# Attention over sixteen images: one image's score chunks, value projection and value products in another order

## The chip, the cores and the metric

The kernel runs on one core of a Trainium2 chip. The time is that of the device for one execution, in microseconds (us); a kernel is run several times and its median is given. A separate execution is recorded by the hardware profiler; it has a time of its own and a span, which is the stretch from the first to the last recorded instruction.

The engines are TensorE (PE in the profile, its weight loads PEld), VectorE (DVE), ScalarE (ACT), GpSimd (POOL) and SyncE (SP, which issues DMAs). Each has a queue of its own.

## What is computed

Four layers follow each other on x of shape (16, 256, 28, 28) in float32. The first is a 3x3 convolution of signs with batch norm, the second a gated block with a 3x3 and a 1x1 convolution, the third has two 3x3 convolutions of signs with batch norms. The change lies in the fourth, an attention within each image, with N = 28 * 28 = 784 positions and 64 reduced channels:

```python
xf = x.reshape(B, C, N)
q = jnp.einsum('rc,bcn->bnr', Wq, xf)
k = jnp.einsum('rc,bcn->brn', Wk, xf)
v = jnp.einsum('rc,bcn->bnr', Wv, xf)
scale = 1.0 / jnp.sqrt(jnp.float32(k.shape[1]))
attn = jnp.einsum('bnr,brm->bnm', q, k) * scale
attn = jax.nn.softmax(attn, axis=-1)
out = jnp.einsum('bnm,bmr->brn', attn, v)
out = jnp.einsum('cr,brn->bcn', Wp, out)
return out.reshape(B, C, H, W) + x
```

## The kernel before

The layers are stages, one after the other on the one core. The images stay in SBUF between the last two stages, as 128 partitions x 2 channel blocks x 784 positions each. The attention is `attend_unshifted` (L1242), some 280 us at the end of the span. It begins with the third layer's last batch norm and activation, which `finish_a` (L1283, ScalarE, with a GpSimd DMA that adds the residual from DRAM) and `finish_b` (L1290, VectorE) apply image by image.

An image's keys are cut into seven chunks of 112 positions, padded to 128 rows. For each chunk, `scores(b, c)` (L1326) multiplies keys by queries with two matmuls of 64 rows, one in the upper and one in the lower half of the array, into a pair of PSUM banks (pool `ps_sc`, two pairs). ScalarE takes the exponential of the 128 x 784 result into one of seven SBUF buffers `es` (L1335). The softmax is not shifted by its maximum.

- `queries_keys` (L1305) makes queries and keys of an image with full 128 x 128 matmuls into the bank pair `mi`; `keys_to` (L1317) and `queries` (L1312) copy them out, on ScalarE and VectorE.
- `project_v` (L1389) makes the values with tiles of 128 rows and 32 columns into bank `sm`; a ScalarE copy goes to `vt`, and `turn_v` (L1403, VectorE) transposes it.
- `values(b, c)` (L1356) multiplies a chunk's exponentials by its values with tiles of 128 x 64, accumulating over the seven chunks in bank `av`. `take_values` (L1364, ScalarE) copies the sum out.
- `sum_up` (L1337) adds exponentials of chunks, those of chunks 0 to 3 on GpSimd and 4 to 6 on VectorE; `sum_all` (L1347, VectorE) joins both; `denominators` (L1369) sums over the partitions by matmuls with ones, again 128 x 64, into bank `sm`; `invert` (L1377) and `normalize` (L1380) are on VectorE. `watch` (L1384, ScalarE) keeps sums for a check of range.
- `project(b, mo)` (L1406) makes one half of the output channels with 64-row matmuls into `mi`, and VectorE adds the result to the image (L1423). `store` (L1443) writes the image out by a DMA of SP.

In the trace one float32 matmul appears as two, so that one score chunk or one half of a projection is x4.

The order on PE, ScalarE, VectorE and GpSimd is that of the calls, written out by hand: `tc.manual_schedule` (L1449) keeps each engine's instructions as the program issues them. The loop over images (L1469) interleaves three images: scores of image b, queries, keys and values of image b + 1, denominators of b - 1 and projections of b - 2. `project(b - 2, ...)` is done only for b > 1, and `take_values(b - 1)` and `denominators(b - 1)` only for b > 0. The last image has its own code (L1520 and below), which stays as it is.

Of the kernel before, what the change touches and what calls it, by code (L numbers as in the profile page):

```python
# [1220 lines left out]
def two_banks(pool, tag):  # L1221
    return pool.tile([P, 2, 512], F32, tag=tag, name=tag)
# [19 lines left out]
def attend_unshifted(ctx, tc, d, out, wqk, wv, wp, keys, worst, doubts, flag, pv, finish):  # L1242
# [31 lines left out]
    def buf(name, bufs, dt=F32, shape=(P, 2, HN)):  # L1274
        return ph.tile(list(shape), dt, tag=name, name=name, bufs=bufs)
# [7 lines left out]
    def finish_a(b, n=slice(0, N), ks=range(2)):  # L1283
        for k in ks:
            v = x[b][:, k, n]
            A.activation(v, v, AF.Identity, bias=bg3[:, k:k + 1], scale=sg3[:, k:k + 1])
        if b >= 2 and 1 in ks:
            nc.gpsimd.dma_start(out=x[b], in_=x2d[b], accum_op=ALU.add)

    def finish_b(b, n=slice(0, N), ks=range(2)):  # L1290
        for k in ks:
            v = x[b][:, k, n]
            if b < 2:
                V.tensor_tensor(v, v, x2[b][:, k, n], ALU.add)
            V.scalar_tensor_tensor(v, v, alpha[:, k:k + 1], v, ALU.mult, ALU.max)  # L1295

    def keep_busy(n):

        ps = one_bank(pssm, "sm")
        for _ in range(n):  # L1300
            T.matmul(ps, lhsT=idle[:, 0:P], rhs=idle, start=True, stop=True)
# [3 lines left out]
    def queries_keys(b, h, ps):  # L1305

        for k in range(2):
            T.matmul(  # L1308
                ps[:, h, :HN], lhsT=wqk[:, k, :], rhs=x[b][:, k, h * HN:(h + 1) * HN], start=(k == 0), stop=(k == 1)
            )  # L1310

    def queries(b, h, ps):  # L1312
        if h == 0:
            qs[b] = buf("q", 2, shape=(P, HN))
        A.copy(qs[b][64 * h:64 * h + 64], ps[0:64, h, :HN])  # L1315

    def keys_to(b, rows, h, ps):  # L1317
        copy = A.copy if rows else V.tensor_copy
        copy(  # L1319
            keys[b % 2][64 * rows:64 * rows + 64, :, 2 * h:2 * h + 2, 0:GC].rearrange("p c g i -> p g c i"),  # L1320
            ps[64:P, h, :HN].rearrange("p (g c i) -> p g c i", g=2, i=GC),
        )
# [3 lines left out]
    def scores(b, c):  # L1326
        ps = two_banks(pssc, "sc")
        chunk = keys[b % 2].rearrange("p c g i -> p c (g i)")[:, c, :]
        for h in range(2):
            rows = slice(64 * h, 64 * h + 64)  # L1330
            T.matmul(  # L1331
                ps[:, h, :HN], lhsT=chunk[rows], rhs=qs[b][rows], start=True, stop=True
            )
        e = es[b, c] = buf("es", 7)
        A.activation(e, ps[:, :, :HN], AF.Exp, scale=0.125)  # L1335

    def sum_up(b, *cs):  # L1337

        for c in cs:
            late, e = c > 3, es[b, c]  # L1340
            if c in (1, 5):
                sums[b, late] = buf(f"sum{c}", 2)
                (V if late else nc.gpsimd).tensor_tensor(sums[b, late], es[b, c - 1], e, ALU.add)
            elif c in (2, 3, 6):
                (V if late else nc.gpsimd).tensor_tensor(sums[b, late], sums[b, late], e, ALU.add)  # L1345
# [18 lines left out]
    def take_values(b, n=slice(0, HN)):  # L1364
        if n.start == 0:
            os[b] = (buf("o", 2, shape=(P, HN)), buf("r", 2, shape=(P, HN)))
        A.copy(os[b][0][:, n], avs[b][:, n])
# [12 lines left out]
    def normalize(b, n=slice(0, HN)):  # L1380
        o, r = os[b]
        V.tensor_tensor(o[:, n], o[:, n], r[:, n], ALU.mult)
# [20 lines left out]
    def turn_v(b):  # L1403
        V.transpose(va[b % 2].rearrange("p c r -> p (c r)"), vt.rearrange("p c a i -> p (c a i)"))
# [38 lines left out]
    def store(b, mo=slice(0, 2), queue=nc.sync):  # L1443
        queue.dma_start(out=out[b][:, mo], in_=x[b][:, mo])
# [4 lines left out]
    with tc.manual_schedule(engines={ET.PE, ET.Activation, ET.DVE, ET.Pool}):  # L1449

        ps = [two_banks(psmi, "mi"), two_banks(pssc, "sc")]
        for h in range(2):
            n = slice(h * HN, h * HN + HN)
            finish_a(0, n)
            finish_b(0, n)
            queries_keys(0, h, ps[h])
        keep_busy(8)
        for h in range(2):
            keys_to(0, 1, h, ps[h])
            queries(0, h, ps[h])  # L1460
            keys_to(0, 0, h, ps[h])
        finish_a(1)
        scores(0, 0)
        project_v(0)
        finish_b(1, ks=(0,))
        turn_v(0)
        finish_b(1, ks=(1,))
        V.transpose(ones.rearrange("p a i -> p (a i)"), turned.rearrange("p a i -> p (a i)"))
        for b in range(B - 1):  # L1469
            scores(b, 1)  # L1470
            if b > 0:
                take_values(b - 1)
            if b == 0:
                finish_a(2)
            if b > 1:
                project(b - 2, 0)()
            sum_up(b, 1)
            scores(b, 2)
            if b > 0:
                sum_up(b - 1, 6)  # L1480
            scores(b, 3)
            sum_up(b, 2, 3)
            ps = two_banks(psmi, "mi")
            for h in range(2):
                queries_keys(b + 1, h, ps)
            for h in range(2):
                keys_to(b + 1, 1, h, ps)
            for h in range(2):
                queries(b + 1, h, ps)
            for h in range(2):  # L1490
                keys_to(b + 1, 0, h, ps)
            project_v(b + 1)
            if b > 0:
                sum_all(b - 1)
            turn_v(b + 1)
            scores(b, 4)
            scores(b, 5)
            sum_up(b, 5)
            if b + 2 < B:
                finish_b(b + 2)  # L1500
            if b + 3 < B:
                finish_a(b + 3)
            for c in range(4):
                values(b, c)
            if b > 0:
                denominators(b - 1)
                invert(b - 1)
                normalize(b - 1)
            scores(b, 6)
            scores(b + 1, 0)  # L1510
            if b > 1:
                project(b - 2, 1)()
                store(b - 2)
            if b > 0:
                watch(b - 1)
            for c in range(4, NC_):
                values(b, c)


        b = B - 1  # L1520
        scores(b, 1)
        take_values(b - 1)
        project(b - 2, 0)()
        sum_up(b, 1)
        scores(b, 2)
        denominators(b - 1)
        invert(b - 1)
        scores(b, 3)
        sum_up(b, 2, 3)
        normalize(b - 1)  # L1530
        scores(b, 4)
        scores(b, 5)
        sum_up(b, 5)
        scores(b, 6)
        project(b - 2, 1)()
        store(b - 2)
        doubts_so_far()
        for mo in range(2):
            project(b - 1, mo, pool=pssc)()
        store(b - 1)  # L1540
        watch(b - 1)
        for c in range(3):
            values(b, c)
        denominators(b)
        for c in range(3, NC_):
            values(b, c)

        parts = [slice(0, HN // 2), slice(HN // 2, HN)]
        os[b] = (buf("o", 2, shape=(P, HN)), buf("r", 2, shape=(P, HN)))
        r = os[b][1]  # L1550
        watched = [worst[:, i:i + 1] for i in range(4 * b, 4 * b + 4)]
        junk = buf("junk", 1, shape=(P, HN))
        A.activation(junk, dns[b], AF.Copy, accum_out=watched[0])
        for n in parts:
            invert(b, n)
        A.activation(junk[:, parts[0]], r[:, parts[0]], AF.Copy, accum_out=watched[1])
        V.tensor_reduce(watched[2], r[:, parts[1]], AX.X, ALU.add)
        A.copy(os[b][0], avs[b][:, :HN])
        up = raise_flag(two_banks(psmi, "mi")[:, 0, :])
        for n in parts:  # L1560
            normalize(b, n)
        up()

        adds = [
            project(b, mo, ps, n) for n, mo, ps in (
                (parts[0], 0, two_banks(psmi, "mi")),
                (parts[0], 1, two_banks(pssc, "sc")),
                (parts[1], 0, [one_bank(pssm, "sm"), one_bank(psav, "av")]),
                (parts[1], 1, two_banks(pssc, "sc")),
            )  # L1570
        ]
        for add in adds[0::2]:
            add()
        store(b, slice(0, 1), nc.scalar)
        for add in adds[1::2]:
            add()
        store(b, slice(1, 2), nc.scalar)
# [178 lines left out]
```

## Time and profile before

| what | value |
|---|---|
| median of 3 runs | 975.81 us (974.52 to 977.21) |
| profiled execution, its own time | 975.5 us |
| its span | 973.7 us |
| mean granted TensorE clock | 0.994 |
| PE busy | 944.8 us (97%) |
| DVE busy | 773.4 us (79%) |
| ACT busy | 722.3 us (74%) |
| POOL busy | 141.0 us (14%) |
| exponentials, L1335 | 112 of 822 ns each |
| score matmuls, L1331 | 448 of 513 ns each, in pairs side by side |
| value and denominator matmuls into `av`, L1352 | 448 of 499 ns each, in pairs |
| reciprocal, L1378, 128x392 | 2608 ns each |

How to read it: a line of the timeline gives the start in us from the span's start, the busy length in us, the engine, the line of the kernel, the operation, the tile that is written and those that are read, the shapes, and how many instructions are merged (x8). For matmuls, "64*128" is the part of the array that one matmul uses, rows times columns. In brackets stands the idle time of that engine just before the group, and what ended it. The ends of matmuls are modelled, and matmuls side by side overlap, so a run of matmuls is best measured from its start to the start of the next run.

### The profile page before, as it was taken

What the parts mean: (1) busy time and instruction counts of PE and PEld (TensorE: products, weight loads), DVE (VectorE), ACT (ScalarE), POOL (GpSimd) and SP (SyncE); (2) the same over time, 40 slices, a digit from 0 to 9 for tenths busy, and PEclk for the clock granted to TensorE, in tenths of its full rate; (3) what the DMA queues carried; (4) which work ended last, traced back from release to release, by engine and by line L of the source; (5) the groups of instructions that cost most, each with busy time, mean ns of one, the idle gap of its engine ahead of it and who ended that gap; (6) DMA issues with size and microseconds to landing.
All of it is one profiled execution on the core that took longest, in us unless ns stands there. A gap on an engine that the chain in (4) does not pass through costs nothing.

```text
span 973.7 us, 14804 instructions
## 1 busy us (share of the span) xinstructions
PE 944.8 (97%) x5615; PEld 582.8 (60%) x5615; DVE 773.4 (79%) x1417; ACT 722.3 (74%) x1199; POOL 141.0 (14%) x149
## 2 busy tenths in 40 slices
PE   7999899999999999999999999999999999999996
PEld 3555568877887878887555555555444444444443
DVE  4767878899998889985799997999757777777765
ACT  6787468888888888874788868887676767666652
POOL 3000100000000000000100000000054444444431
PEclk9999999999999999999999999999999999999998
DMA  9877513334443222110490000000044353525212
GB/s 347 312 271 270 197 50 99 116 115 131 146 152 117 100 100 96 58 63 34 180 383 1 1 1 1 1 1 1 1 71 96 72 129 70 130 67 133 67 67 103
DMA packets 26948, 105.82 MB, mean 109 GB/s; under 512 B 3490, under 2 KB 7268, under 8 KB 26868
## 3 DMA queue, kind: packets, MB, share of 16 engines
q1 hardware_dynamic: 20948, 73.44, 21.2%
q0 software_dynamic: 5632, 30.54, 11.6%
q8 instruction: 46, 0.75, 0.3%
q10 hardware_dynamic: 288, 0.80, 0.2%
q14 instruction: 34, 0.28, 0.1%
HBM read 72.67 MB, written 32.11 MB: 108 GB/s over the span
## 4 chain that ended last, share of the span: by engine, by line
PE 46%; DVE 3%; ACT 1%; issue 1%; DVEq 0%; ACTq 0%
PE cv L340 19%; PE sc L1331 8%; PE av L1352 8%; PE mi L1308 4%; PE sm L1394 2%; PE mi L1412 2%; PE sm L1352 1%; DVE p L1118 1%; DVE ab L354 0%; ACT es L1335 0%; DVE l2b_fin L1120 0%; DVE l2c_fin L1120 0%; DVE r L1378 0%; DVE p L1295 0%; PE sc L1412 0%
## 5 line engine op out<-in xcount | busy, mean ns | idle before, releaser
L340 PE MATMUL cv<-fpads,wpk 128*128 128x392 f16 (+1 forms) x1746 | 295.7, 331 | 10.2 <-ACT fpads L451 5.0
L713 PE MATMUL cv<-vs,w 128*128 128x392 bf16 (+1 forms) x1536 | 287.1, 356 | 2.9 <-DVE vs L134 2.7
L340 PEld LDWEIGHTS <-wpk 128*128 128x128 f16 x1746 | 169.0, 97 | 137.3 <-issue 9.9
L713 PEld LDWEIGHTS cv<-vs,w 128*128 128x128 f32 x768 | 142.6, 190 | 11.7 <-ACT vs L695 0.7
L1335 ACT ACTIVATE es<-sc 128x784 f32<-128x784 f32 x112 | 87.3, 822 | 41.4 <-PE sc L1331 41.4
L713 PEld LDWEIGHTS <-w 128*128 128x128 f16 x768 | 67.7, 101 | 58.1 <-issue 18.5
L1331 PE MATMUL sc<-q,keyswa 64*128 64x392 f32 x448 | 89.9, 513 | 0.9 <-ACT es L1335 0.9
L1118 DVE SCALAR_TENSOR_TENSOR p<-ab,vec 128x392 f32<-128x392 f32 x128 | 79.1, 618 | 2.3
L1352 PE MATMUL av<-es,v 128*64 128x392 f32 x448 | 80.7, 499 | 0.0
L1345 POOL TENSOR_TENSOR sum<-sum,es 128x784 f32<-128x784 f32 x32 | 67.2, 2100 | 3.1 <-ACT es L1335 0.6
L1331 PEld LDWEIGHTS sc<-q,keyswa 64*128 64x128 f32 x448 | 38.9, 186 | 44.0 <-issue 17.1
L851 POOL DMA_DIRECT2D x2d<-x x16 | 8.6, 537 | 343.9 <-DVE x L845 280.9
L1319 DVE COPY keyswa<-mi 64x392 f32<-64x392 f32 x31 | 16.3, 564 | 52.6 <-ACT q L1315 52.5
L1352 PEld LDWEIGHTS av<-es,v 128*64 128x64 f32 x448 | 29.4, 136 | 47.4 <-issue 47.0
L695 ACT CAST vs<-vs 128x840 fp32r<-128x840 bf16 x64 | 54.7, 882 | 1.5 <-DVE vs L134 1.5
L351 ACT ACTIVATE t<-cv,rounding 128x392 f32<-128x392 f32 (+2 forms) x82 | 51.6, 630 | 4.9 <-PE cv L340 1.9
L1123 ACT ACTIVATE t<-ab 128x392 f32<-128x392 f32 x64 | 33.5, 524 | 27.9 <-DVE ab L354 27.9
L823 PE MATMUL cv<-z,fw 128*128 128x392 f32 x256 | 48.9, 342 | 1.0 <-ACT z L815 0.8
L354 DVE SCALAR_TENSOR_TENSOR ab<-ab,cv 128x392 f32<-128x392 f32 x64 | 35.5, 554 | 17.5 <-ACT ab L352 17.5
L823 PEld LDWEIGHTS cv<-z,fw 128*128 128x128 f32 x256 | 45.7, 188 | 2.3 <-ACT z L815 2.1
L1308 PE MATMUL mi<-p,wqk 128*128 128x392 f32 x124 | 45.3, 506 | 0.3 <-DVE p L1295 0.3
L432 PE MATMUL unused<-idle 128*128 128x512 bf16 x175 | 40.5, 389 | 3.0 <-POOL idle L468 3.0
(287 smaller groups left out, 1511.4 us busy)
## 6 DMA issues: line engine op xcount, KB each, us to landing
xs<-in_x_dram SPq DMA_DIRECT2D x30, 784.0 KB, 5.8
x2d<-x POOLq DMA_DIRECT2D x16, 784.0 KB, 3.8
out_dram<-p SPq DMA_DIRECT2D x15, 784.0 KB, 3.8
p<-x2d POOLq DMA_DIRECT2D x14, 784.0 KB, 6.9
p<-x2d SPq DMA_DIRECT2D x13, 784.0 KB, 16.1
n0d<-n POOLq DMA_DIRECT2D x16, 392.0 KB, 4.7
n<-n0d SPq DMA_DIRECT2D x16, 392.0 KB, 3.3
st<-in_w_dram SPq DMA_DIRECT2D x12, 384.0 KB, 6.1
```

Of the source, the lines that this page charges most:

```text
L340: T.matmul(pss[j][:, n // size if careful else h, :rows * S].rearrange("p (a b) -> p a b", b=S), lhsT=w[:, n, t, :], rhs=pads[:, blocks[j] ...
L351: A.activation(by_halves(t, blocks[j]), ps, AF.Identity, bias=rounding, scale=1.0 / PACK)
L432: tc.keep_in_program_order(T.matmul(ps, lhsT=idle[:, 0:P], rhs=idle, start=True, stop=True))
L695: A.copy(v, w)
L713: T.matmul(ps.rearrange("p (a b) -> p a b", b=S), lhsT=w[:, k, c, u, mo * P:(mo + 1) * P], rhs=v[:, b % 2, u, k, :, c:c + S], start=(n == ...
L823: T.matmul(ps[:, h, :HN], lhsT=w[:, k, mo * P:(mo + 1) * P], rhs=z2[b][:, k, h * HN:(h + 1) * HN], start=(k + i == 0), stop=(k + i == 2),)
L1118: V.scalar_tensor_tensor(p, y, alpha[:, mo:mo + 1], y, ALU.mult, ALU.max)
L1308: T.matmul(ps[:, h, :HN], lhsT=wqk[:, k, :], rhs=x[b][:, k, h * HN:(h + 1) * HN], start=(k == 0), stop=(k == 1))
L1331: T.matmul(ps[:, h, :HN], lhsT=chunk[rows], rhs=qs[b][rows], start=True, stop=True)
L1335: A.activation(e, ps[:, :, :HN], AF.Exp, scale=0.125)
L1345: (V if late else nc.gpsimd).tensor_tensor(sums[b, late], sums[b, late], e, ALU.add)
L1352: T.matmul(ps[64 * h:64 * h + 64, :HN], lhsT=w, rhs=e[:, h, :], start=start, stop=stop)
```

## The change

Only the order of calls in the loop over the images changes. Chunk 4's scores move from behind `turn_v` to the score chunks 1 to 3; chunk 2's scores move ahead of the first projection; chunk 5's scores move behind the denominators, to chunk 6; the second projection moves between chunk 6's scores and the next image's chunk 0; `sum_up(b, 5)` moves behind that projection. So no scores stand any more between the value projection and the value products. Calls, buffers and shapes are the same.

```diff
             if b == 0:
                 finish_a(2)
+            scores(b, 2)
             if b > 1:
                 project(b - 2, 0)()
             sum_up(b, 1)
-            scores(b, 2)
+            scores(b, 3)
             if b > 0:
                 sum_up(b - 1, 6)
-            scores(b, 3)
+            scores(b, 4)
             sum_up(b, 2, 3)
             ps = two_banks(psmi, "mi")
...
             if b > 0:
                 sum_all(b - 1)
             turn_v(b + 1)
-            scores(b, 4)
-            scores(b, 5)
-            sum_up(b, 5)
             if b + 2 < B:
                 finish_b(b + 2)
             if b + 3 < B:
                 finish_a(b + 3)
             for c in range(4):
                 values(b, c)
             if b > 0:
                 denominators(b - 1)
                 invert(b - 1)
                 normalize(b - 1)
+            scores(b, 5)
             scores(b, 6)
-            scores(b + 1, 0)
             if b > 1:
                 project(b - 2, 1)()
                 store(b - 2)
+            sum_up(b, 5)
+            scores(b + 1, 0)
             if b > 0:
                 watch(b - 1)
             for c in range(4, NC_):
                 values(b, c)
```

## The prediction

> **What bounds the kernel now.** I read the windows first. From 737.58 to 934.47 us, twelve images of the attention, TensorE is busy for the whole stretch, at full clock; VectorE (DVE), ScalarE (ACT) and GpSimd (POOL) have room.
>
> ```profile
> 737.58:934.47 196.89, 196.89 (x1298) 91.57 (x1297) 146.62 (x144) 132.17 (x226) 83.81 (x48) 1.00 0.38 95
> ```
>
> The columns are length, busy time of PE, PEld, DVE, ACT and POOL, clock, DMA share, GB/s. A busy PE can still be slow where one kind of matmul follows another, so I then read PE's timeline over one image. A run ends where the next line starts; the second column overlaps the next run a little.
>
> ```profile
> 797.52 0.93 PE L1331 MATMUL sc<-q,keyswa 64*128 64x392 f32 x4
> 798.29 0.84 PE L1412 MATMUL mi<-o,wp 64*128 64x392 f32 x4
> 798.96 1.48 PE L1331 MATMUL sc<-q,keyswa 64*128 64x392 f32 x8
> 800.37 2.90 PE L1308 MATMUL mi<-p,wqk 128*128 128x392 f32 x8
> 803.21 1.53 PE L1394 MATMUL sm<-p,wv 128*32 128x196 f32 x32
> 804.67 1.59 PE L1331 MATMUL sc<-q,keyswa 64*128 64x392 f32 x8
> 806.19 2.85 PE L1352 MATMUL av<-es,v 128*64 128x392 f32 x16
> 808.87 0.83 PE L1352 MATMUL sm<-sum,ones 128*64 128x392 f32 x4
> 809.63 1.59 PE L1331 MATMUL sc<-q,keyswa 64*128 64x392 f32 x8
> 811.05 0.82 PE L1412 MATMUL mi<-o,wp 64*128 64x392 f32 x4
> 811.80 2.19 PE L1352 MATMUL av<-es,v 128*64 128x392 f32 x12
> ```
>
> x4 is one score chunk (or one half of a projection), x8 two, in the tiling written as rows*columns. The next image begins at 813.93: 16.41 us each. There are seven runs of one tiling: 64*128, 128*128, 128*32, 64*128, 128*64, 64*128, 128*64.
>
> Third, ACT over the same image, because each score chunk needs an exponential before its bank pair is free again, and there are two pairs.
>
> ```profile
> 798.50 0.82 ACT L1335 ACTIVATE es<-sc 128x784 f32<-128x784 f32 x1 [0.51 <-PE sc L1331]
> 799.22 0.48 ACT L1367 COPY o<-av 128x392 f32<-128x392 f32 x1
> 799.89 1.54 ACT L1335 ACTIVATE es<-sc 128x784 f32<-128x784 f32 x2 [0.19 <-PE sc L1331]
> 803.31 0.87 ACT L1319 COPY keyswa<-mi 64x392 f32<-64x392 f32 x2 [1.88 <-PE mi L1308]
> ```
>
> Between the exponentials of chunks 1 and 2 stands the copy of the last image's values (take_values). It costs nothing now: exponential 2 starts 0.19 us late only for want of its scores.
>
> Fourth, images 0 and 1, the only places where PE waits for an exponential: two lines of PE, then ACT for image 0 and for image 1.
>
> ```profile
> 703.14 0.93 PE L1331 MATMUL sc<-q,keyswa 64*128 64x392 f32 x4 [0.27 <-ACT es L1335]
> ...
> 718.16 0.93 PE L1331 MATMUL sc<-q,keyswa 64*128 64x392 f32 x4 [0.33 <-ACT es L1335]
> ```
>
> ```profile
> 702.27 0.82 ACT L1335 ACTIVATE es<-sc 128x784 f32<-128x784 f32 x1 [0.30 <-PE sc L1331]
> 702.99 1.96 ACT L1286 ACTIVATE p<-p,l2c_c,l2c_r 128x784 f32<-128x784 f32 x2
> 704.85 1.52 ACT L1335 ACTIVATE es<-sc 128x784 f32<-128x784 f32 x2
> ...
> 717.28 0.82 ACT L1335 ACTIVATE es<-sc 128x784 f32<-128x784 f32 x1 [2.16 <-PE sc L1331]
> 718.00 0.48 ACT L1367 COPY o<-av 128x392 f32<-128x392 f32 x1
> 718.36 1.65 ACT L1335 ACTIVATE es<-sc 128x784 f32<-128x784 f32 x2
> ```
>
> These give the price of a wait. The exponential of 717.28 ends at 718.10; the third chunk starts at 718.16, 0.05 us later, and the queries-and-keys run at 719.01: 0.86 us from a chunk that waited to the next run, 0.75 (766.81 to 767.56) from one that did not. An exponential starts 0.98 us after the first chunk of a run. The next instruction follows it 0.72 us on, and the exponential behind the copy 0.36 us after the copy's start.
>
> **What the Trainium skill says.** TensorEngine Tiling (Array Packing), Key Properties: changing the tiling mode, not just the tile, drains TensorE. The trace agrees: at a change of tiling the weight loads stop for 0.56 to 0.61 us (0.31 after 128*32). TensorE: Matmul & The Clock Gate, Architectural detail: ACT and DVE are strictly first in, first out. So exponential 2 cannot pass the copy; ACT's timeline has the kernel's order. ScalarE: Activation LUTs, What ACT_TABLE_LOAD costs: back-to-back ACTIVATEs overlap by about 93 ns; here an exponential of 0.82 us is followed after 0.72.
>
> **The change, part by part.**
>
> *One run fewer.* Chunk 4 joins chunks 1 to 3, chunk 5 joins 6 and the next image's 0. Runs: scores 1, 2, project, 3, 4; queries and keys; v; values 0-3 and denominators; scores 5, 6, project, scores 0; values 4-6. Six tilings, not seven; the matmuls are the same. Inside a run a chunk costs 0.655 us (both projection and chunk), so two cost 1.31, and the run that goes takes 1.52 (804.67 to 806.19): 0.21 us is its own entry and exit. The v run (1.46 against eight steps of 0.164, or 1.31) and the values run (3.44 with denominators against ten of 0.328, or 3.28) carry 0.15 and 0.16 and now meet each other. 128*32 to 128*64 is not in the trace. If it needs no drain, about 0.16 more goes; if it drains as the others, nothing. The skill's sentence speaks for the drain: I take -0.21 per image, ends -0.37 and -0.16.
>
> *A fourth chunk in the run.* Count from chunk 1's start in images 2 to 14. PE: chunk 2 at 0.77, project 1.43, chunk 3 2.09, chunk 4 2.75. ACT: exponential 1 at 0.98, copy 1.70, exponential 2 at 1.70 + 0.36 = 2.06, its end 2.88. Chunk 3 needs exponential 1 (ends 1.80): no wait, as now. Chunk 4 needs exponential 2: it starts at 2.93, and the next run at 2.93 + 0.86 = 3.79 instead of 2.85 + 0.655 = 3.51. The wait costs 0.28 (0.38 if exponential 2 comes 0.46 after the copy, as the exponential after the vt copy does at 805.18 and 805.64). Per image: -0.21 + 0.28 = +0.07, 16.48 us; thirteen images, +0.9.
>
> *Image 1* has no first project to give ACT time. Chunk 3 waits as it does now; exponential 2 ends at 719.18, chunk 4 starts 719.23, the next run 720.09, where it was 719.01: +1.08. The 1.52 run goes. Scores 5, 6, 0 have no project either (b > 1 guards it): chunk 0 waits for exponential 5, at 0.98 + 0.82 + 0.05 = 1.85, plus 0.86 = 2.71 instead of 1.52: +1.19. Sum +0.75.
>
> *Image 0* has two 128x784 affine passes (finish_a(2)) between exponentials 1 and 2: exponential 2 starts at 704.85, ends 705.6, chunk 4 starts 705.67, the next run 706.53 instead of 704.00: +2.53. With -1.52 and +1.19: +2.20. PE is busy from there to 934 us, so nothing later swallows this.
>
> *What else moves.* sum_up(b, 5) (0.93 us on DVE) goes behind the reciprocal (2.61), normalize and project's addition: they start 0.85 earlier in DVE's queue, good for the "mi" bank, which project 0 and then queries-and-keys wait for. Project 0's addition ends near 3.3, before 3.79. sum_up(b, 5) ends about 1.5 us into the next image; its first reader, sum_up(b, 6), and the buffer reuse by exponential 4 (near 4.0) are later: zero. finish_a(b + 3), off ACT's two exponentials, lets POOL issue its DMA 1.5 us earlier; POOL's sums end before it (801.35 + 4.40 = 805.75); nothing reads that image before the next. SP's store stays behind project 1. ACT is free for the key copies: exponential 4 ends 0.93 us after queries-and-keys starts, the copies wait until 2.94. Cost zero each.
>
> *The wait that gets tight.* Denominators need sum_all(b - 1), which stays where it was (ends 807.12, or 6.75 us after queries-and-keys starts), while PE reaches them 1.52 us earlier, at 2.84 + 1.46 + 2.68 = 6.98. About 0.1 us is left after the weight load. Behind that matmul all of PE is queued. I take zero; 0.2 us at the other end.
>
> *Sum:* 0.9 + 0.75 + 2.20 = 3.9 us. The profiled execution took 975.5 us (span 973.7 and 1.8 around it): 979.4. The median is 0.3 above that: **979.7 us**, own range 978.5 to 981.
>
> **Rivals.**
> - *Denominators late* (DVE, sum_all): for it, the 0.1 us margin; against it, a projection whose weight load waits 0.38 us for DVE (814.61) costs nothing visible. 0.2 us in 14 images, +2.8: 982.5.
> - *No drain between v and values*: for it, both tilings use all 128 rows; against it, the skill. 0.16 in 15 images, -2.4: 977.3.
> - *Not slower: the copy does not hold chunk 4 back.* Exponential 2 would have to end by 2.70, 0.18 earlier, so that chunk 4 stands only behind PE; images 2 to 14 then bring -0.21 x 13 = -2.7 against +2.95 of the first two: 976.1, no change. For it: ACT idles 0.5 us before exponential 1; against it: that idling is for PE, and the copy's time is measured. It decides from a wait under 0.21 us.
> - That the order is not what the lines say is excluded: the built program has it so.
>
> **How the numbers follow.** Forecast 0.50, late denominators 0.20, no drain 0.18, no wait 0.08, further stalls 0.02, a gain of a kind I don't see 0.02. 0.3%, or 2.9 us, is about what can be told from no change: slower means over 978.7. Of the forecast some 0.42 lies above that; with late denominators and further stalls, slower is 0.64. Same is the rest of the forecast (0.08), no wait (0.08) and no drain but for its edge (0.17): 0.33. Faster is that edge and the unseen gain, 0.03. The range, 977.0 to 983.0, leaves out the no-wait case, the lower part of no-drain, and the far tail, under 2 in 10.
>
> **What would show it.** In the new profile: an idle entry before one score chunk per image "<-ACT es", near 0.2 us in images 2 to 14, above 1 us in image 0; a period of 16.48; v to values 1.46 us. Wrong if the period is below 16.3 (no wait or no drain), if PE waits for "DVE sum" at the denominators, or if the first two images don't lose about 3 us.

## The result and the profile after

The kernel after takes 979.25 us (median of 6 runs, 978.13 to 980.77), the kernel before, run beside it, 975.30 us (6 runs, 974.41 to 977.21). The ratio is 1.0039, with a 95% interval of 1.0025 to 1.0052: slower by 2.4 to 5.1 us. The profiled execution of after took 980.77 us, with a span of 979.0 us.

The windows first. These are the twelve images that the prediction showed of before, from the second chunk of image 2 to that of image 14; the columns are length, busy time of PE, PEld, DVE, ACT and POOL, clock, DMA share and GB/s.

```profile
736.30:934.48 198.18, 197.54 (x1299) 92.37 (x1297) 138.14 (x144) 134.07 (x227) 83.77 (x47) 1.00 0.37 91
```

196.89 us have become 198.18, that is 16.515 us for each image instead of 16.41. PE is still busy but for 0.64 us, so the shares of busy time tell nothing here; the length of each run does. PE over one image:

```profile
802.36 1.59 PE L1331 MATMUL sc<-q,keyswa 64*128 64x392 f32 x8
803.78 0.82 PE L1412 MATMUL mi<-o,wp 64*128 64x392 f32 x4
804.44 1.81 PE L1331 MATMUL sc<-q,keyswa 64*128 64x392 f32 x8
806.17 2.90 PE L1308 MATMUL mi<-p,wqk 128*128 128x392 f32 x8
809.01 1.53 PE L1394 MATMUL sm<-p,wv 128*32 128x196 f32 x32
810.47 2.85 PE L1352 MATMUL av<-es,v 128*64 128x392 f32 x16
813.15 0.83 PE L1352 MATMUL sm<-sum,ones 128*64 128x392 f32 x4
813.91 1.59 PE L1331 MATMUL sc<-q,keyswa 64*128 64x392 f32 x8
...
816.75 2.19 PE L1352 MATMUL av<-es,v 128*64 128x392 f32 x12
818.87 1.59 PE L1331 MATMUL sc<-q,keyswa 64*128 64x392 f32 x8
```

There are six runs now. From start to start they take 3.81, 2.84, 1.46, 3.44, 2.84 and 2.12 us. The first of them holds chunks 1 to 4, and its last pair of chunks shows 1.81 us of busy time where an undisturbed pair, in the prediction's lines of before, shows 1.48: 0.33 us of waiting. Since matmuls overlap in the record, only 0.05 us of it is idle time of PE itself, too short to be listed. It is listed at the weight loads, of which the fourth chunk's is:

```profile
805.31 0.30 PEld L1331 LDWEIGHTS sc<-q,keyswa 64*128 64x128 f32 x4 [0.68 <-ACT es L1335]
```

That load unit stood idle for 0.68 us, until an exponential on ACT ended. Which one, ACT shows over the same stretch:

```profile
803.34 0.82 ACT L1335 ACTIVATE es<-sc 128x784 f32<-128x784 f32 x1 [0.53 <-PE sc L1331]
804.06 0.48 ACT L1367 COPY o<-av 128x392 f32<-128x392 f32 x1
804.42 2.69 ACT L1335 ACTIVATE es<-sc 128x784 f32<-128x784 f32 x3
```

Exponential 1, then the copy, then exponentials 2 to 4 in one row. Exponential 2 starts at 804.42, 0.36 us after the copy's start, and ends at 805.26; the weight load of chunk 4 starts at 805.31. In the kernel before, exponential 2 had an idle entry of 0.19 us behind the copy (for PE's scores); here its scores are ready and it starts as soon as the copy lets it. At this exponential ACT has become what PE waits for. Exponentials 3 and 4 wait for their own scores again: they start 0.11 and 0.10 us after the one before has ended, too little to be listed, and the row of three takes 2.69 us where three back to back would take about 2.26 (0.82 and twice 0.72).

Images 0 and 1, the chunks whose matmuls wait:

```profile
706.97 0.93 PE L1331 MATMUL sc<-q,keyswa 64*128 64x392 f32 x4 [1.64 <-ACT es L1335]
...
716.80 0.93 PE L1331 MATMUL sc<-q,keyswa 64*128 64x392 f32 x4 [0.31 <-issue]
...
721.70 0.93 PE L1331 MATMUL sc<-q,keyswa 64*128 64x392 f32 x4 [0.33 <-ACT es L1335]
722.81 0.93 PE L1331 MATMUL sc<-q,keyswa 64*128 64x392 f32 x4 [0.17 <-ACT es L1335]
...
733.32 0.93 PE L1331 MATMUL sc<-q,keyswa 64*128 64x392 f32 x4 [0.33 <-ACT es L1335]
```

Image 0's chunk 4 (706.97) waits 1.64 us for the exponential behind the two affine passes. Chunk 0 of images 1 and 2 (716.80, 733.32) waits for exponential 5 of the image before; the profile names "issue" at the first of them, but both start right behind that exponential, 0.09 and 0.05 us after its end (716.71, 733.26). The first two images, from chunk 1 of image 0 to chunk 1 of image 2, take 33.75 us (702.55 to 736.30) where they took 30.62 (701.29 to 731.91).

So the 5.3 us between the two spans divide as follows: 4.53 in the attention's loop from image 0 to image 15, of which 3.13 in the first two images and 1.40 in the other thirteen; 1.26 ahead of it, where both kernels are alike; and -0.52 behind it. The 1.26 is scatter between executions: in the twelve profiled executions here the first chunk 1 stands anywhere from 700.0 to 703.0 us. The end scatters too: TensorE's last projections ran for the most part at a granted clock of 0.5 in some executions (the one of before) and at 1.0 in others (the one of after). The clock goes with the time of whole executions: of the 35 of before that ran beside the first experiments, the 16 with a mean granted clock of 0.997 or more took 973.48 to 976.11 us, the 19 with a lower one 975.64 to 977.88. So the experiments below are read by the period of the loop first and by the median second.

### The profile page after: what moved, and what is told of

The parts are those of the page before. It is cut to its first block, busy times and chain, and to the rows that moved or that the text cites. A ratio compares the mean times of both kernels' runs of the same rounds, so it can differ in the third digit from the quotient of the medians.

```text
span 979.0 us, 14825 instructions
## 1 busy us (share of the span) xinstructions
PE 946.9 (97%) x5609; PEld 583.6 (60%) x5615; DVE 764.6 (78%) x1417; ACT 724.7 (74%) x1199; POOL 141.0 (14%) x149
## 4 chain that ended last, share of the span: by engine, by line
PE 43%; ACT 4%; DVE 3%; issue 1%; DVEq 0%; ACTq 0%
PE cv L340 19%; PE av L1352 8%; PE sc L1331 7%; PE mi L1308 4%; ACT es L1335 2%; PE sm L1394 2%; PE sm L1352 1%; PE mi L1412 1%; DVE p L1118 1%; ACT o L1367 1%; DVE ab L354 0%; DVE l2b_fin L1120 0%; DVE l2c_fin L1120 0%; DVE r L1378 0%; ACT p L1286 0%
## 5 line engine op out<-in xcount | busy, mean ns | idle before, releaser
L1335 ACT ACTIVATE es<-sc 128x784 f32<-128x784 f32 x112 | 90.5, 825 | 49.8 <-PE sc L1331 47.1
L1331 PE MATMUL sc<-q,keyswa 64*128 64x392 f32 x448 | 92.7, 514 | 4.1 <-ACT es L1335 3.0
L1343 POOL TENSOR_TENSOR sum<-es 128x784 f32<-128x784 f32 x16 | 30.0, 1876 | 100.7 <-ACT es L1335 100.7
```

Source lines behind the costliest of these rows:

```text
L1331: T.matmul(ps[:, h, :HN], lhsT=chunk[rows], rhs=qs[b][rows], start=True, stop=True)
```

## The experiments

The theory: the run that goes saves 0.2 us, and a new wait of PE for exponential 2, which stands on ScalarE behind the copy (and in image 0 behind the affine passes), costs more. Each edit is against the kernel after unless another is named.

**The copy behind exponential 2; images 0 and 1 in the old order; both.**

```diff
             scores(b, 1)
-            if b > 0:
-                take_values(b - 1)
             if b == 0:
                 finish_a(2)
             scores(b, 2)
+            if b > 0:
+                take_values(b - 1)
```

> The changed kernel, with the copy of the last image's values (take_values) behind the exponential of chunk 2 instead of ahead of it on ScalarE. Theory (the copy holds chunk 4 back): exponential 2 starts 1.70 us after chunk 1 instead of 2.06 and ends at 2.52, before chunk 4 is due at 2.75; the wait of 0.3 us goes in images 2 to 14 and most of it in image 1, the period falls from 16.51 to 16.20 us: 979.3 - 13 x 0.31 - 0.4 = 974.9 us, beside 975.3 of the kernel before. Rival (four chunks against two bank pairs are too many, since an exponential takes 0.72 us and a chunk 0.655, wherever the copy stands): the wait only shrinks by a part, period 16.4 and 977.5 us or more. Rival (the loss is not in these waits but in a run that is longer or in the stages ahead): 979 us.

Measured: 975.59 us; to before (975.98 beside it) 0.9998, interval 0.9986 to 1.001. ACT in images 2 to 14 is now in the order exponentials 1 and 2, copy, exponentials 3 and 4:

```profile
801.40 1.54 ACT L1335 ACTIVATE es<-sc 128x784 f32<-128x784 f32 x2 [0.53 <-PE sc L1331]
802.84 0.48 ACT L1367 COPY o<-av 128x392 f32<-128x392 f32 x1
803.44 1.54 ACT L1335 ACTIVATE es<-sc 128x784 f32<-128x784 f32 x2
```

The first run takes 3.49 us instead of 3.81, the busy time of the last two chunks is 1.48 again, and the period is 16.19 (784.24 to 800.43): 0.32 less per image. One instruction of 0.48 us, moved by one place on an engine that is busy for only 68% of this stretch (134.07 of 198.18 us in after), gives back about as much as the change cost.

For images 0 and 1 the loop's body is that of before, for the others that of after:

```diff
         for b in range(B - 1):
-            scores(b, 1)
...
+            if b < 2:
+                scores(b, 1)
...
+            else:
+                scores(b, 1)
...
```

> The changed kernel, with images 0 and 1 in the order of the kernel before, so that only images 2 to 14 have the new order. Theory: the first two images lose 3.1 us in the changed kernel and this takes it back: 979.3 - 3.1 = 976.2 us, the period of the later images still 16.51. Rival (the loss is spread evenly over the images): 979.3 - 2 x 0.3 = 978.7 us.

Measured: 975.95 us, 1.0007 (0.9999 to 1.0016). From chunk 1 of image 0 to chunk 1 of image 2 it is 30.62 us (700.87 to 731.49), the figure of before to the hundredth, and the period behind it stays at 16.51. So the loss of the first two images is 3.1 us, and it changes nothing in the period of the images behind them.

> Both edits: images 0 and 1 in the order of before, the copy behind exponential 2 in the others. Theory: only the gain of one run fewer is left, 13 x 0.21 = 2.7 us under the kernel before: 972.6 us, ratio to before 0.997, period 16.20. Rival (one tiling change fewer is worth nothing, the time that the matmuls wait for a drain comes back elsewhere): 975.3 us, period 16.41.

Measured: 971.92 us (6 runs, 970.76 to 973.05), 0.9962 (0.9946 to 0.9977). Period 16.19, first two images 30.62; from image 0 to image 15 the loop takes 241.09 us, 2.81 less than in before, where 2.7 were forecast. **This version beats both kernels**: the change's order with the copy one place later, and from image 2 on. Its median is lower by more, 4.1 us, but not all of that is the order: all its six executions had a mean granted clock of 0.997 or more, and the 16 of before with such a clock have a median of 974.28, 2.4 us above it.

**The copy twice: in after and in before.** The second copy goes to a scratch buffer that nobody reads.

```diff
         A.copy(os[b][0][:, n], avs[b][:, n])
+        A.copy(buf("junk", 1, shape=(P, HN))[:, n], avs[b][:, n])
```

> The changed kernel, with a second copy of the same values (128x392, into a scratch tile) right behind the first, ahead of exponential 2. Theory: in images 1 to 14 exponential 2 and chunk 4 come one copy later, 0.36 to 0.46 us: 979.3 + 14 x 0.4 = 984.9 us (984.3 to 985.7), period 16.9. Rival (ScalarE is idle a quarter of the time, the copy is not on the path): 979.3 us.

Measured in after: 987.08 us, 1.0119 (1.0097 to 1.0141). The second copy starts 0.36 us after the first, exponential 2 starts 0.38 us after the second, and the fourth chunk's wait becomes visible on PE itself:

```profile
789.59 0.93 PE L1331 MATMUL sc<-q,keyswa 64*128 64x392 f32 x4 [0.44 <-ACT es L1335]
```

The period is 16.90, 0.39 more; from image 0 to image 15 the loop takes 253.90 us, 5.46 more than after (14 copies of 0.39). What the median has beyond the forecast, some 2 us, the profiled execution shows in the end: the last projections, at a granted clock of 0.5, took 2.89 us to the store's issue against 1.93 in after, and the last store landed 4.45 us after its issue against 3.43.

> The kernel before, with the second copy (128x392, into a scratch tile) right behind the first. Theory: there exponential 2 has no chunk 4 of the same run behind it, the next run is queries and keys, which needs no exponential; the same copy that costs 0.39 us per image in the changed kernel costs nothing here: 975.3 us, period 16.41. Rival (ScalarE's extra time is paid anywhere): 975.3 + 14 x 0.39 = 980.8 us.

Measured in before: 977.26 us, 1.0015 (1.0006 to 1.0024). The loop from image 0 to image 15 takes 243.93 us, in before 243.91; the period is 16.41. So the same copy costs 5.5 us in the one order and nothing in the other. What the median shows beside before (975.04), some 2 us, does not lie in the loop. The profiled execution has its excess of 1.84 us behind the loop: 0.29 ahead of the last projections, 0.46 in them, and 1.10 behind the issue of the last store, which landed after 4.46 us as in the experiment before (3.36 to 3.50 in the ten other profiled executions). In part the executions differ in their clock: twelve of eighteen had a mean below 0.997, of before nine of 26. At 0.997 and more the medians are 974.96 and 974.80; below it they are 977.58 and 976.42. Whether the second copy causes what is left was not shown.

**The denominators' sum earlier.**

```diff
             for h in range(2):
                 queries(b + 1, h, ps)
+            if b > 0:
+                sum_all(b - 1)
             for h in range(2):
                 keys_to(b + 1, 0, h, ps)
             project_v(b + 1)
-            if b > 0:
-                sum_all(b - 1)
```

> The changed kernel, with sum_all ahead of the second pair of key copies on VectorE, so that the denominators' input is ready some 4 us earlier. Theory: the denominators had 0.1 us to spare and did not wait; no change: 979.3 us, period 16.51, only the late weight load at the denominators (idle 0.40) goes back to 0.19. Rival (denominators late): 0.1 us in 14 images or more, 977.9 us or less.

Measured: 979.55 us, 1.004 (1.0026 to 1.0053), period 16.51. In after, the weight load of the denominators does stand 0.40 us idle, where those ahead of it stand 0.19, and it starts 0.11 us after the sum's end:

```profile
813.04 0.26 PEld L1352 LDWEIGHTS sm<-sum,ones 128*64 128x64 f32 x4 [0.40 <-issue]
```

```profile
811.96 0.97 DVE L1348 TENSOR_TENSOR sum<-sum,sum 128x784 f32<-128x784 f32 x1
```

With the sum early that gap is gone, and the period is the same:

```profile
811.27 0.14 PEld L1352 LDWEIGHTS sm<-sum,ones 128*64 128x64 f32 x2 [0.18 <-issue]
```

So the 0.2 us by which the load was late lay inside its lead over the matmul. The rival of the late denominators is out.

**Seven runs again, without the waits.** From the version of both edits, chunk 4 is put back behind the turn of v for images 2 to 14:

```diff
-                scores(b, 4)
                 sum_up(b, 2, 3)
...
                 turn_v(b + 1)
+                scores(b, 4)
```

> The kernel with both edits (images 0 and 1 as before, the copy behind exponential 2), with chunk 4's scores put back between the value projection and the value products in images 2 to 14: seven tilings again, the rest of the order as in the changed kernel. Theory (the gain is one change of tiling fewer, 0.21 us per image): period 16.41, 13 x 0.21 = 2.7 us more than with six runs, 974.6 to 975.3 us. Rival (the gain comes from where the copy, the projection and the sums stand): period 16.20 stays, 971.9 us.

Measured: 982.34 us, 1.0069 (1.0056 to 1.0082): a miss by 7 us. The period is 16.88, not 16.41, and that makes 6.1 of the 7 us (13 times 0.47). PE and DVE, in this order:

```profile
802.89 2.90 PE L1308 MATMUL mi<-p,wqk 128*128 128x392 f32 x8 [0.42 <-DVE p L1423]
```

```profile
801.86 0.97 DVE L1423 TENSOR_TENSOR p<-mi,p 128x784 f32<-128x784 f32 x1 [1.68 <-PE mi L1412]
```

Queries-and-keys needs the bank pair "mi", which the addition of project 0 empties at 802.83. That projection stands behind chunk 2 now; chunks 3 and 4 together cover its addition, chunk 3 alone does not. So the chunk that the change brings into the run has a second effect that the forecast of this experiment overlooked: it is what allows the projection to stand so late. To test this, the projection alone goes back ahead of chunk 2:

```diff
+                if b > 1:
+                    project(b - 2, 0)()
                 scores(b, 2)
                 if b > 0:
                     take_values(b - 1)
-                if b > 1:
-                    project(b - 2, 0)()
```

> The seven-run order of the last-but-two experiment (four scores chunk behind the turn of v's tiling, the copy behind exponential 2, images 0 and 1 in the old order) with one line moved: project(b-2, 0) ahead of scores(b, 2), as the kernel before has it, for images 2 to 14. My theory: that run lost 0.47 us per image because the projection stood behind chunk 2 and its addition on VectorE was covered by chunk 3 alone; with the projection one chunk earlier the addition ends before queries-and-keys is due, the wait of 0.42 us on line 1308 goes, the period returns from 16.88 to about 16.41 us and the time from 982.3 to about 975 to 976 us. Rival: the place of chunk 4 itself costs it (an own run of the scores and a later exponential 4): then the period stays near 16.88 and the time near 982.

Measured: 975.47 us, 0.9999 (0.9988 to 1.001), period 16.39 (797.32 to 813.71). The wait is gone, as forecast:

```profile
800.15 2.90 PE L1308 MATMUL mi<-p,wqk 128*128 128x392 f32 x8
```

And 16.39 with seven runs against 16.19 with six, neither with a wait on PE, makes the price of a run 0.20 us per image.

**Image 0's affine passes behind chunk 4.**

```diff
             if b > 0:
                 take_values(b - 1)
-            if b == 0:
-                finish_a(2)
             scores(b, 2)
...
             scores(b, 4)
+            if b == 0:
+                finish_a(2)
```

> The changed kernel, with image 0's two affine passes (finish_a(2)) behind the exponential of chunk 4 instead of ahead of that of chunk 2. Theory: chunk 4 of image 0 then waits only for exponential 2 right behind exponential 1, at 2.6 us after chunk 1 instead of 4.4: 1.8 to 1.9 us less, 977.4 us, the other images unchanged; the DMA that adds image 2's residual goes out later, which only VectorE feels. Rival (image 0's loss is hidden by later waits, or moves to image 2's residual that comes too late): 979.3 us or more.

Measured: 980.58 us, 1.0046 (1.0033 to 1.0058): no gain in the median. The wait of chunk 4 is gone, queries-and-keys starts 3.42 us after chunk 1 instead of 5.28. But then it waits, once, for `finish_b(1)`. PE, DVE and GpSimd:

```profile
707.88 2.24 PE L1308 MATMUL mi<-p,wqk 128*128 128x392 f32 x6 [0.48 <-DVE p L1295]
```

```profile
705.28 2.54 DVE L1295 SCALAR_TENSOR_TENSOR p<-p,vec 128x784 f32<-128x784 f32 x1
```

```profile
704.92 2.06 POOL L1343 TENSOR_TENSOR sum<-es 128x784 f32<-128x784 f32 x1 [14.50 <-ACT es L1335]
```

The DVE instruction takes 2.54 us where it took 1.03 in after, beside a GpSimd sum. In after that sum began only at 707.11, since the DMA issue of `finish_a(2)`, waiting for the affine passes, stood ahead of it in GpSimd's queue; moved back, it lets the sum begin behind exponential 1 at once. From chunk 1 of image 0 to that of image 1 it is 16.14 us against 17.24: 1.10 us of the 1.85 are saved, 0.75 go into this new wait and the restart behind it. The median hides even that. The last projections of the profiled execution ran at a granted clock of 0.5 (969.89 to 973.30), and all six executions had a mean clock of 0.991 to 0.995, where those of after had 0.995 to 0.997.

**Four runs.** An own version: all seven chunks in one run, project 0 behind chunk 1 and project 1 behind chunk 3; then queries-and-keys, v, and all value products with the denominators among them. The cut shows the scores and projections; smaller moves of the sums and in the last image's code go with them.

```diff
+                scores(b, 0)
+            scores(b, 1)
...
+            scores(b, 2)
             scores(b, 3)
...
+            if b > 1:
+                project(b - 2, 1)()
+                store(b - 2)
+            scores(b, 4)
+            scores(b, 5)
+            sum_up(b, 5)
+            scores(b, 6)
+            if b > 0:
+                take_values(b - 1)
...
-            scores(b, 5)
-            scores(b, 6)
-            if b > 1:
-                project(b - 2, 1)()
-                store(b - 2)
-            sum_up(b, 5)
-            scores(b + 1, 0)
```

> An own version with four tilings per image: all seven scores chunks of an image in one run with both projections between them (0, 1, project 0, 2, 3, project 1, 4, 5, 6), then queries-and-keys, v, values 0 to 3, denominators of the image before, values 4 to 6; the copy of the image's values behind its exponential 6. My theory, that the price of a run (0.2 us and more) and the waits of chunks on exponentials are what the order decides: 6.13 + 2.84 + 1.46 + 5.41 = 15.84 us per image against 16.41 before, some 0.57 for 14 images, 967 to 968 us. Rival: chunks come every 0.66 to 0.82 us and exponentials every 0.72, so ScalarE falls behind in the long run, or the additions of the two projections on VectorE come late for queries-and-keys: waits ahead of the later chunks or of line 1308, a period of 16.2 or more, and 972 us or more.

Measured: 984.61 us, 1.0093 (1.0078 to 1.0108), period 16.96 (798.45 to 815.41): the rival's side. Two waits on PE:

```profile
800.32 0.93 PE L1412 MATMUL mi<-o,wp 64*128 64x392 f32 x4 [0.28 <-DVE o L1382]
...
804.84 0.93 PE L1331 MATMUL sc<-q,keyswa 64*128 64x392 f32 x4 [0.27 <-ACT es L1335]
```

There are two runs fewer than in after, and the three short ones take 9.71 us together (805.70 to 815.41), as worked out. The long run takes 7.25 instead of 6.13. Project 0 starts 1.87 us after chunk 0, where the third step of the same run in after starts after 1.42 (803.78 less 802.36), since normalize, behind the reciprocal of 2.61 us, ends only at 800.27. And chunk 6 starts 1.75 us after chunk 4 instead of 1.31: it needs the bank pair of chunk 4, which comes free when that exponential ends, and it waits as the third of three chunks in a row did in images 0 and 1 of before. Together 0.89 of the 1.12 us; the rest comes with the restarts after a wait, 0.76 instead of 0.66 us to the next chunk and 0.86 instead of 0.75 to the next run. This version was not taken further.

## Why the prediction was right

Forecast 979.7, measured 979.25; the range and the likeliest case held. By its own steps:

- *One run fewer, -0.21 us.* Right: -0.20, as 16.19 against 16.39 with no wait in either. "If it drains as the others, nothing": from the start of v to the start of the run behind it is 1.46 us in after, where the values follow, as in before, where scores followed, so 128*32 to 128*64 costs what 128*32 to 64*128 cost. This agrees with what the Trainium skill says in TensorEngine Tiling (Array Packing), Key Properties, that changing the mode drains TensorE. The rival in which this pair is cheaper is out.
- *The wait of the fourth chunk, +0.28.* Right in kind, a little small: 0.32 (16.51 against 16.19 with the copy behind exponential 2). Chunk 4 starts 2.95 to 2.96 us after chunk 1 (forecast 2.93), and the run would have taken 3.49 without the wait, not 3.51. Period 16.515, forecast 16.48; for thirteen images 1.40 us, forecast 0.9. The range's other end, 0.38, was not reached. The sign that the prediction named, an idle entry near 0.2 us at PE, did not appear in images 2 to 14: the entry stands at the weight load, with 0.68. That the copy is the reason is shown from both sides: behind exponential 2 it costs nothing, doubled it costs 0.39 per image, doubled in before nothing.
- *Image 1, +0.75, and image 0, +2.20.* Measured +0.84 and +2.29. Image 0 is the chunk-4 wait of 2.57 (forecast 2.53), the run saved and chunk 0's wait of 1.23 (forecast 1.19). The old order in these images alone gives back the 3.1 us.
- *The sum, 3.9 us.* In the loop it is 4.53; the medians differ by 3.95. The agreement of the medians is partly luck: the parts of the forecast are all too small (0.9 for 1.40, 0.75 for 0.84, 2.20 for 2.29), and the ends of the executions scatter by more than the difference of 0.6.
- *What else moves, zero.* Project 0's addition ended near 3.3 us as forecast (805.62 less 802.36 is 3.26), ahead of queries-and-keys. The profile names this addition at the weight load of queries-and-keys (0.56 us idle, as at other changes of tiling), but it is not what that run waits for: with the copy behind exponential 2 the addition ends at the same 3.26 us and the run starts 0.32 us earlier, at 3.49. The zero holds because chunk 4 stands there: without it, in the seven-run order, the same addition costs 0.49 us per image (16.88 against 16.39). The prediction gave the time but did not say that chunk 4 covers it.
- *Denominators, zero.* Right: the load came late, the matmul did not.
- *Rival "not slower".* It needed a wait under 0.21 us, and the wait is 0.32. With the copy behind exponential 2 the wait is gone, and the time is close to what this rival named: 975.59 against its 976.1.

What stays open: the 0.75 us of image 0 that went to GpSimd and DVE were not recovered in another order, why TensorE's clock differs at the end of executions was not studied, and what lies behind the late landing of the last store in both kernels with a second copy is not known.

## What to carry to other kernels

Where a group of instructions is joined to save a change of tiling, work out for each member which buffer it needs and which instruction of the other engine frees it, counted from the run's start; what stands ahead of that instruction in its first-in, first-out queue decides, and not the engine's share of busy time. Then look at what the joined members cover and uncover: here the same move bought 0.2 us per image and sold 0.32, and the best order measured was the change with one copy moved by one place, from image 2 on. Count the first rounds of a loop by themselves, since the work that gives the others slack is not there yet.

## What the runs showed of the hardware

The Trainium skill's page SBUF — State Buffer, section SBUF: two separate sides, says that a VectorE instruction with two SBUF inputs and a GpSimd instruction that reads SBUF share a port pair under an exclusive lock: whichever starts first has it to its end. The traces agree with the order in which they run, and add a time. A VectorE sum or scaling of 128x784 with two SBUF inputs, about 1 us alone, that starts beside a GpSimd sum ends 0.83 or 0.84 us after that sum's end, in all 181 such cases in the traces of the twelve kernels. Four of them: at 806.95 for 806.12 in after (1.41 us long), at 802.11 for 801.27 in before (2.04 us), at 807.82 for 806.98 with the affine passes late (2.54 us), at 807.67 for 806.84 with four runs (2.14 us). So the cost grows with what remains of the GpSimd instruction, up to 1.5 us here (2.54 against 1.03), and a change that moves an exponential, on which the GpSimd sum waits, can move this cost too.

The granted clock of TensorE fell to 0.5 near the end of every profiled execution, but not at the same place: at 965.1 us in before, among the last projections, and at 976.4 in after, behind the last matmul. The first four matmuls of the last projections took 0.60 us in after, at 1.00, and 1.03 us in before with the second copy, at 0.50.
